# A transformer block in fp32 on one core: the chunk order of a softmax batch, the turn of one output tile, and the queue that issues half of the block swaps

## The chip, the cores and the metric

The kernel runs on one core of a Trainium2 chip. Time is device time in microseconds for one launch, smaller is better; the figure compared is the median of several runs.

## What is computed

An adaptive-layernorm block on x of 2048 rows and 512 columns, all in float32. A vector c gives six modulation rows (shift, scale and gate for each half). The first half is causal attention with 16 heads of 128; the second is a shared gated MLP plus a mixture of 64 experts, of which each row takes 4 (at most 128 rows per expert).

```python
mod = (silu(c) @ wmod).reshape(1, 6, 1, -1)
sa, ca, ga, sb, cb, gb = ...            # ga, gb kept at least 0.25 away from 0
h = layernorm(x) * (1 + ca) + sa
q, k, v = h @ Q_w + Q_b, h @ K_w + K_b, h @ V_w + V_b      # per head
x = x + ga * (softmax(causal(q @ k.T / sqrt(128))) @ v @ O_w + O_b)
h = layernorm(x) * (1 + cb) + sb
x = x + gb * (experts(h, top 4 of softmax(h @ Wr + router_bias)) + shared_mlp(h))
```

## The kernel before

The attention stage fills the span from about 54 us to 1658 us. The 2048 query rows are 16 tiles of 128 rows; two neighbours form a pair, 0 to 7. Pair pr needs 2*pr+1 and 2*pr+2 key blocks of 128. The pairs of a head are worked in five batches, `BATCHES = ((7,), (6,), (5, 0), (4, 1), (3, 2))`, so there are 16 x 5 = 80 steps, written (head, batch) below.

A batch passes through four phases, which are spread over three steps:

- Softmax (`softmax_tile`). A tile's row of logits is cut into chunks of at most 1024 columns. A chunk (pair, tile, number) is multiplied on TensorE (L572) into a PSUM tile `ps`, of which there are two in a ring (tag "sc"). VectorE adds the causal mask to the last 128 columns (L584) and takes the negative maximum (L585; L589 joins that of a tile's first chunk). ScalarE writes the exponential into `p` (L591). When a tile is complete, `normalise` makes its factor (L547 to L554); the scaling itself is done on VectorE (L559, only in batches 0 and 1 for the pair's first tile) or ScalarE (L795). `CHUNKS` lists the order of a batch's chunks.
- Swap (`swap_blocks`, L616). The 32-row groups of `p` are moved to other partitions, as 16 DMAs from SBUF to SBUF of 104 to 124 KB, into a tile `pt`. Part a of `pt`, a = 0 to 3, is written by four of the DMAs; those of parts 0 and 1 are issued first (`half` 0), then those of parts 2 and 3 (`half` 2). `p` and `pt` have two buffers each.
- Turn (`turn_blocks`, L626). VectorE transposes the 32 x 32 blocks of part a in place. There are four turns per batch.
- Weighted values (`weighted_values`, L644). TensorE multiplies the values with `pt` into `po`; ScalarE adds the bias into `at` (L653, one buffer), and GpSimd's queue (POOL) stores it to DRAM as `atd` (L658).

In step n TensorE works on the weighted values of batch n, on the softmax of batch n+2 and on fill work: the q and k products of the next head (`project`, L222) and the value products of the next group (`values`, L447). `merge` writes these streams out as one order by hand: it always takes the next item of the stream whose done share is smallest, and at given shares of the whole it inserts marks. The turns of batch n+1 are the marks 0.58, 0.66, 0.8 and 0.88. The swap of batch n+2 is issued when the step's streams are at their end:

```python
for a, at in enumerate((0.58, 0.66, 0.8, 0.88)):
    marks.append((at, lambda a=a: turn(n + 1, a)))
merge([st for st in streams if st], marks)
if n + 2 < len(steps):
    swap(n + 2)
```

So the softmax of batch 3 (pairs 4 and 1, the first "mixed" row that the change touches) is worked in step (head, 1), and that of batch 2 (pairs 5 and 0) in step (head, 0). Every engine runs its instructions in the order in which they are written. All loads of weights, the swaps and the reloads of `atd` are issued from SP's queue; POOL's queue has the stores of `atd` and of the normed rows, and later the gathers of the expert stage.

The output stage follows (tiles t of 128 rows, 1658 us to about 1830 us). For each tile TensorE adds up 16 products, one per head (L1140); VectorE adds the result to the residual (L1163), and `norm(t)` makes the normed rows h: statistics (L955, L957), square root on ScalarE (L959), then L960 to L966. `turn_h(t)` transposes h on TensorE (L973) and copies it on ScalarE (L974) into `h2T`; `logit(t)` multiplies that with the router's weights (L982); `choose` makes the routing of two tiles. The dictionaries `TURN`, `LOGIT` and so on say after which product (t, hd) of the loop each of these is written. In that loop a `TURN` stands ahead of a `norm` at the same place. `norm(1)`, `norm(2)` and `norm(3)` are written at (4,10), (4,12) and (4,15), `norm(4)` at the end of tile 4, `logit(0)` at (4,14) and `logit(1)` at (5,3).

The expert stage and the shared MLP follow; the change does not touch them.

Of the kernel before, what the change touches and what calls it, by code (L numbers as in the profile page):

```python
# [23 lines left out]
def adaln_block_kernel(  # L24
# [23 lines left out]
    nc = tc.nc  # L48
# [74 lines left out]
    with ExitStack() as att:  # L123
# [386 lines left out]
        def blocks_of(s):  # L510
            return sum(4 * pr + 3 for pr in BATCHES[s])

        def first_block(s, pr):
# [8 lines left out]
            ((7, 1, 0), (7, 1, 1), (7, 0, 0), (7, 0, 1)),  # L522
            ((6, 1, 0), (6, 1, 1), (6, 0, 0), (6, 0, 1)),
            ((5, 0, 0), (0, 0, 0), (5, 0, 1), (5, 1, 0), (0, 1, 0), (5, 1, 1)),
            ((4, 1, 0), (4, 1, 1), (1, 0, 0), (4, 0, 0), (4, 0, 1), (1, 1, 0)),
            ((3, 1, 0), (2, 1, 0), (3, 0, 0), (2, 0, 0)),
        )

# [80 lines left out]
        def swap_blocks(s, pb):  # L609

            w = blocks_of(s) * 32
            pt = ptp.tile([P, PW], F32, name="pt")
            for half, d in [(h, d) for h in (0, 2) for d in range(4)]:
                for a in (half, half + 1):
                    b = (a + d) % 4
                    nc.sync.dma_start(  # L616
                        out=pt[32 * b : 32 * (b + 1), a * w : (a + 1) * w],
                        in_=pb[32 * a : 32 * (a + 1), b * w : (b + 1) * w],
                    )
            return pt  # L620
# [189 lines left out]
        def swap(n):  # L810
            flush()
            flush_shares()
            turned[n] = swap_blocks(steps[n][1], probs.pop(n))
# [156 lines left out]
    def turn_h(t):  # L970
        tp = psO.tile([P, DC, P], F32, name="tp", tag="tr")
        for k in range(DC):
            nc.tensor.transpose(tp[:, k, :], hs_[t][:, k * P : (k + 1) * P], ident)  # L973
        nc.scalar.copy(h2T[:, :, t * P : (t + 1) * P], tp)  # L974
# [122 lines left out]
    table = psO.tile([CAP, 2 * E], F32, name="table", tag="tr")  # L1097
    ALL = ((0, 4), (4, 8), (8, 12), (12, 16))

    TURN = {(4, 10): 0, (5, 0): 1, (5, 4): 2, (5, 9): 3, (6, 1): 4, (6, 8): 5}  # L1100
    LOGIT = {(4, 14): 0, (5, 3): 1, (5, 15): 2, (6, 2): 3, (6, 11): 4, (6, 15): 5}
    POSITION = {(5, 14): 0, (6, 10): 1}
    SEAT = {(6, 5): 0, (7, 0): 1}
    for t in range(7, NT):
        TURN[t, 10] = t - 1
        LOGIT[t, 14] = t - 1
# [4 lines left out]
    with tc.manual_schedule():  # L1111
# [17 lines left out]
        for t in range(NE, NT):  # L1129
# [9 lines left out]
            for hd in range(H):  # L1139
# [7 lines left out]
                if hd == 5:  # L1147
                    nc.vector.tensor_add(acc[:, t, :], acc[:, t, :], ga)
                if (t, hd) in TURN:
                    turn_h(TURN[t, hd])  # L1150
                if (t, hd) in ((4, 10), (4, 12), (4, 15)):
# [419 lines left out]
```

## Time and profile before

| | |
|---|---|
| median of 3 runs | 2384.27 us (2384.24 to 2387.44) |
| the profiled execution | 2396.46 us, span 2394.7 us, granted clock 0.995 |
| TensorE (PE) busy | 2339.7 us, 98% |
| VectorE (DVE) busy | 1548.9 us, 65% |
| ScalarE (ACT) busy | 861.7 us, 36% |
| GpSimd (POOL) busy | 218.9 us, 9% |
| swap DMAs (L616) | 1280, all on SP's queue |
| stores of `atd` (L658) | 128 on POOL's queue |
| DMA queue q1 (SP), q0 (POOL) | 252.74 MB and 54.54 MB |

In the rows of the profile a group is named by line, engine, operation and tiles, output first. A timeline row begins with its start and its duration in us, and in square brackets stand the idle time of its engine before it and what ended that. PEld is TensorE's weight load, SPq and POOLq are the queues' own instructions. The waits list says who waited for whom: total us, times, longest. A share of busy time is a mean over the stages of the span.

### The profile page before, as it was taken

The page shows a single profiled execution, that of the slowest core. Times are in us where ns is not written, and L with a number is a line of the kernel's source. Part 1 is how long each engine was busy: PE and PEld are TensorE (multiplying, and loading weights), DVE is VectorE, ACT ScalarE, POOL GpSimd, SP SyncE. Part 2 cuts the span into 40 slices and gives each one's busy share as a digit, 9 for nine tenths or more (in the row PEclk, how much of TensorE's full clock was granted, in tenths as well). Part 3 has the DMA queues.
Part 4 walks back from the last instruction along what each step waited for, and adds up shares of the span by engine and source line. Part 5 has one row for each costly group of instructions (what it writes and reads, how often), then busy time and mean ns, then how long its engine had stood idle before and what let it go on. Part 6 is the DMA issues. An engine that isn't in the chain of part 4 may idle for free.

```text
span 2394.7 us, 27691 instructions
## 1 busy us (share of the span) xinstructions
PE 2339.7 (98%) x9078; PEld 1504.3 (63%) x9078; DVE 1548.9 (65%) x3100; ACT 861.7 (36%) x1703; POOL 218.9 (9%) x286
## 2 busy tenths in 40 slices
PE   7999999999999999999999999999999999999989
PEld 3666657666576676666766767555444677867734
DVE  5467767677676776776767767764755654634645
ACT  3344444444444444444444444442111222212200
POOL 0000000000000000000000000000000111211163
PEclk9999999999999999999999999999999999999999
DMA  4234544454454454454544445656232578777564
GB/s 141 64 83 117 126 115 115 101 133 112 96 141 104 104 130 97 119 128 99 120 100 116 114 96 147 190 159 195 78 119 84 154 216 245 232 225 239 169 188 135
DMA packets 223835, 325.84 MB, mean 136 GB/s; under 512 B 31894, under 2 KB 138442, under 8 KB 223692
## 3 DMA queue, kind: packets, MB, share of 16 engines
q1 hardware_dynamic: 196812, 252.74, 41.0%
q0 software_dynamic: 17664, 54.54, 7.5%
q10 hardware_dynamic: 9216, 16.78, 1.9%
q8 instruction: 73, 1.20, 0.2%
q14 instruction: 70, 0.57, 0.1%
HBM read 139.39 MB, written 41.95 MB: 76 GB/s over the span
## 4 chain that ended last, share of the span: by engine, by line
PE 86%; DVE 4%; SPq 3%; issue 2%; ACT 1%; DMA 1%; DVEq 0%; ACTq 0%
PE po L644 17%; PE ps L572 17%; PE pqk L222 13%; PE pv L447 7%; PE pso L1140 6%; PE pst L1289 5%; PE pse L1433 5%; PE psd L1351 5%; PE psg L1205 3%; SPq L616 3%; PE psy L1454 2%; PE psb L769 2%; DVE pt L626 1%; PE tpx L1426 1%; PE pv L497 1%
## 5 line engine op out<-in xcount | busy, mean ns | idle before, releaser
L591 ACT ACTIVATE p<-ps,nm 128x1024 f32<-128x1024 f32 (+7 forms) x384 | 331.7, 864 | 854.1 <-DVE nm L589 359.8
L644 PE MATMUL po<-pt,v 128*128 128x256 f32 (+1 forms) x2304 | 564.8, 368 | 3.0 <-DVE pt L626 2.3
L644 PEld LDWEIGHTS po<-pt,v 128*128 128x128 f32 x2304 | 420.9, 191 | 204.6 <-issue 158.0
L572 PE MATMUL ps<-kt,qt 128*128 128x512 f32 (+3 forms) x1280 | 532.2, 530 | 15.2 <-ACT p L591 14.5
L585 DVE TENSOR_REDUCE nm<-ps 128x1 f32<-128x1024 f32 (+7 forms) x384 | 349.9, 911 | 105.5 <-PE ps L572 96.7
L626 DVE STREAM_TRANSPOSE pt<-pt 128x832 f32<-128x832 f32 (+2 forms) x320 | 337.0, 1069 | 21.8 <-DMA pt<-p 16.1
L572 PEld LDWEIGHTS ps<-kt,qt 128*128 128x128 f32 x1280 | 234.9, 190 | 178.4 <-issue 144.0
L795 ACT ACTIVATE p<-p,rs 128x1024 f32<-128x1024 f32 (+3 forms) x320 | 266.0, 860 | 5.3 <-DVE rs L554 5.1
L658 POOL DMA_DIRECT2D atd<-at x128 | 74.3, 584 | 1584.1 <-ACT at L653 1561.2
L1140 PE MATMUL pso<-hT,T 128*128 128x512 f32 x384 | 175.0, 601 | 0.0
L222 PE MATMUL pqk<-T,sw 128*128 128x512 f32 x360 | 169.2, 592 | 0.0
L584 DVE TENSOR_TENSOR ps<-ps,causal 128x128 f32<-128x128 f32 x256 | 72.8, 284 | 111.5 <-PE ps L572 109.7
L1433 PE MATMUL pse<-wgu,xbT 128*128 128x256 f32 x512 | 121.1, 379 | 0.0
L1140 PEld LDWEIGHTS pso<-hT,T 128*128 128x128 f32 x384 | 70.0, 191 | 71.9 <-issue 71.2
L222 PE MATMUL pqk<-hT,wq 128*128 128x512 f32 x240 | 112.8, 592 | 0.0
L1351 PE MATMUL psd<-wsd,hs 128*128 128x512 f32 x256 | 111.5, 592 | 0.0
L222 PEld LDWEIGHTS pqk<-T,sw 128*128 128x128 f32 x360 | 68.4, 190 | 54.1 <-issue 50.2
L1433 PEld LDWEIGHTS pse<-wgu,xbT 128*128 128x128 f32 x512 | 93.8, 190 | 11.7 <-issue 1.0
L1416 POOL DMA_INDIRECT xb<-h2d,tok x64 | 65.0, 1015 | 297.9 <-PE tpx L1426 275.3
L1428 ACT COPY xbT<-tpx 128x512 f32<-128x512 f32 x64 | 37.3, 585 | 145.7 <-DVE y L1456 56.2
L447 PEld LDWEIGHTS pv<-sgb,T 128*128 128x128 f32 x672 | 81.6, 192 | 8.1 <-issue 6.7
L1351 PEld LDWEIGHTS psd<-wsd,hs 128*128 128x128 f32 x256 | 48.6, 190 | 59.0 <-issue 58.6
(423 smaller groups left out, 2648.2 us busy)
## 6 DMA issues: line engine op xcount, KB each, us to landing
pt<-p SPq DMA_DIRECT2D x768, 104.0 KB
pt<-p SPq DMA_DIRECT2D x256, 124.0 KB
pt<-p SPq DMA_DIRECT2D x256, 108.0 KB
atd<-at POOLq DMA_DIRECT2D x128, 128.0 KB
wgu<-in_L_ffn_Wg_dram SPq DMA_DIRECT2D x64, 256.0 KB
wgu<-in_L_ffn_Wu_dram SPq DMA_DIRECT2D x64, 256.0 KB
wd<-in_L_ffn_Wd_dram SPq DMA_DIRECT2D x64, 256.0 KB
ybd<-y ACTq DMA_DIRECT2D x64, 256.0 KB
```

What stands on the lines that cost most here:

```text
L222: nc.tensor.matmul(out=ps, lhsT=l[:, k], rhs=r[:, k], start=(k == 0), stop=(k == 1))
L447: nc.tensor.matmul(out=ps[:, n], lhsT=l[:, k, n * P : (n + 1) * P], rhs=r[:, k], start=(k == 0), stop=(k == 1),)
L572: nc.tensor.matmul(out=ps[:, o : o + wo], lhsT=q, rhs=kts[hd, (c0 + o) // 512][:, :wo], start=True, stop=True,)
L585: nc.vector.tensor_reduce(nm[:, n : n + 1], ps[:, :w], AX.X, ALU.max, negate=True)
L591: nc.scalar.activation(rows[:, r0 + c0 // P : r0 + (c0 + w) // P], ps[:, :w].rearrange("q (r b k) -> q r b k", b=4, k=32), AF.Exp, bias=nm ...
L626: nc.vector.transpose(part, part)
L644: nc.tensor.matmul(out=po if wide else po[:, P:], lhsT=vts[g, kt // 4][:, kt % 4, hh * DH : (hh + 1) * DH], rhs=rows[:, r : r + last + 1 : ...
L795: nc.scalar.activation(part, part, AF.Identity, scale=r)
L1140: nc.tensor.matmul(out=ps, lhsT=abs_[pr][:, hd, i * P : (i + 1) * P], rhs=wos[hd // 4][:, hd % 4, :], start=(hd == 0), stop=(hd == H - 1),)
L1289: nc.tensor.matmul(out=ps[:, h], lhsT=w[:, k, :], rhs=x_[:, k, :], start=k == 0, stop=k == 1,)
L1351: nc.tensor.matmul(out=ps, lhsT=hsh[b, f][:, i * P : (i + 1) * P], rhs=wsd[:, f, :], start=(f == 0), stop=(f == NHC - 1),)
L1433: nc.tensor.matmul(out=ps, lhsT=xts[e][:, k, :], rhs=weights[e][:, k].rearrange("p i h -> p (i h)"), start=(k == 0), stop=(k == DC - 1),)
```

## The change

Three edits.

- In `CHUNKS` the chunks of pair 4 in the batch (4, 1) begin with the pair's first tile instead of its second. The widths of the row, in order, are 1024, 256, 384, 1024, 128, 512 before and 1024, 128, 384, 1024, 256, 512 after; the latter are those of the batch (5, 0).
- In `swap_blocks` the eight DMAs that write parts 2 and 3 are issued from GpSimd's queue, the other eight from SP's as before.
- In `TURN` tile 1 is transposed at (4, 15), after the last product of tile 4, instead of at (5, 0), after the first product of tile 5.

```diff
-            ((4, 1, 0), (4, 1, 1), (1, 0, 0), (4, 0, 0), (4, 0, 1), (1, 1, 0)),
+            ((4, 0, 0), (4, 0, 1), (1, 0, 0), (4, 1, 0), (4, 1, 1), (1, 1, 0)),
...
             for half, d in [(h, d) for h in (0, 2) for d in range(4)]:
+                queue = nc.sync if half == 0 else nc.gpsimd
                 for a in (half, half + 1):
                     b = (a + d) % 4
-                    nc.sync.dma_start(
+                    queue.dma_start(
                         out=pt[32 * b : 32 * (b + 1), a * w : (a + 1) * w],
                         in_=pb[32 * a : 32 * (a + 1), b * w : (b + 1) * w],
                     )
...
-    TURN = {(4, 10): 0, (5, 0): 1, (5, 4): 2, (5, 9): 3, (6, 1): 4, (6, 8): 5}
+    TURN = {(4, 10): 0, (4, 15): 1, (5, 4): 2, (5, 9): 3, (6, 1): 4, (6, 8): 5}
```

## The prediction

> **What bounds the kernel now.** I read the page first, then TensorE's waits, then the timeline around the longest of them. In the page:
>
> ```profile
> PE 2339.7 (98%) x9078; PEld 1504.3 (63%) x9078; DVE 1548.9 (65%) x3100; ACT 861.7 (36%) x1703; POOL 218.9 (9%) x286
> ...
> PE 86%; DVE 4%; SPq 3%; issue 2%; ACT 1%; DMA 1%; DVEq 0%; ACTq 0%
> ```
>
> TensorE is busy 98% and carries 86% of the chain, so an edit can only win time in which TensorE stands still. Its own waits (engine, line, releaser: total us, times, longest):
>
> ```profile
> PE ps L572 <- ACT p L591: 14.5, 16, 1.5
> ...
> PE pl L982 <- ACT h2T L974: 3.4, 2, 3.2
> ```
>
> The first comes once per head (0.8 in most windows of 100 us), the second once in the output stage. The others that the change can reach are "po L644 <- DVE pt L626" (2.3, once) and "po L644 <- issue" (0.7, once). Together 20.9 us: that is the ceiling, unless a slower step hides more. A cross-check from the chain: per head 14 L222 products at 1.72, 7 L447 products at 1.78, 17408 softmax columns at 1.72 per 1024 and L644 at 0.43 per wide and 0.22 per narrow entry (64 and 8) make 95.0 us; heads repeat every 96.28 (POOL's L658 issue at 970.74 and 1067.02). So 1.3 us per head is idle, of which 0.83 is this wait.
>
> The wait in step (4,1) (head 4, batch 1; its softmax stream works for batch 3 of the same head), from the timeline:
>
> ```profile
> 536.35 0.39 PE L572 MATMUL ps<-kt,qt 128*128 128x128 f32 x2
> ...
> 537.22 1.03 DVE L626 STREAM_TRANSPOSE pt<-pt 128x832 f32<-128x832 f32 x1
> ...
> 538.18 0.27 DVE L584 TENSOR_TENSOR ps<-ps,causal 128x128 f32<-128x128 f32 x1
> ...
> 539.00 0.37 ACT L591 ACTIVATE p<-ps,nm 128x128 f32<-128x128 f32 x1 [4.64 <-DVE nm L589]
> ...
> 539.51 1.99 PE L572 MATMUL ps<-kt,qt 128*128 128x512 f32 x4 [0.83 <-ACT p L591]
> ```
>
> The 128-wide chunk (4,0,1) is multiplied at 536.35, but its mask waits on VectorE behind the third product's add (L240) and the fourth transpose (537.22). Its ps buffer, one of two, is free only after the exponential, and the next step's first chunk stands 0.83 us at 539.51.
>
> **Part A, the order of widths.** No instruction is added or removed; six chunks change places. `merge` takes the stream with the smallest done share. The chunks are 1024, 256, 384, 1024, 128, 512 before; the fifth comes due at 2688/3328 = 0.808 of its stream, after the fifth product (0.8) and after all four turns (marks 0.58 to 0.88). After, 1024, 128, 384, 1024, 256, 512 put it at 2560/3328 = 0.769: ahead of the fifth product, the third and the fourth turn. The sixth stays at 0.846.
>
> Rebuilt from the durations above: TensorE starts the 256-wide chunk (4,1,1) at 534.63 - 0.22 = 534.41 and has it at 535.0. VectorE has done two turns and L236 by 535.0, then mask 0.27, maximum 0.42, minimum 0.16: 535.9. ScalarE's exponential and sum, 0.47 + 0.19, free the buffer at 536.6. TensorE comes to the next step after 0.43 + 1.72 + 0.43 + 0.86 + 0.65: 538.5. So 1.9 us of slack stand where 0.83 was short. Step (4,0) already runs these widths: its 256-wide chunk is at 513.98, its exponential at 516.42, the next step's chunk at 518.51 with no wait. The other buffers of the ring have over 1 us. The last scaling before the block swap is 128 columns wider, about 0.1 us of ScalarE, which is 36% busy. Typical waits alone give 16 x 0.83 = 13.3, the row 14.5. I take 14.0.
>
> **Part B, the queues.** Sixteen block transfers per step stay, in the same sizes. SP issues 16 in 10.0 to 10.8 us (0.63 each); now it issues 8 in 5.1, and POOL the 8 that fill parts 2 and 3. POOL's are queued behind the step's atd issue (L658), which waits for the same weighted sums; the next atd issue, 17 to 20 us later, stands behind them and nothing else does until then. SP's later items (weights, wmod, atd reloads) start some 5 us sooner. Step (4,4):
>
> ```profile
> 581.90 1.35 DVE L559 TENSOR_SCALAR p<-p,rs 128x1024 f32<-128x1024 f32 x2
> 582.09 1.28 POOL L658 DMA_DIRECT2D atd<-at  x2 [16.11 <-ACT at L653]
> ...
> 583.39 10.03 SPq L616 DMA_DIRECT2D pt<-p  x16
> ```
>
> POOL is free at 583.37 when SP starts at 583.39; elsewhere it is at most 0.6 us behind (atd until 565.98, SP from 565.36). POOL's price for a swap is not in the trace. Nearest row: a direct copy on POOL takes 539 ns, two in a row 1.07 us. Other end: an indirect gather comes every 1.25 us (0.95 + 0.30 between). I take the direct copy's, 0.54 to 0.6, since a swap is direct; 1.25 stays as the far end. Landing: a pair of atd issues on POOL ended at 1653.73 and SP, which waited for the second, went on at 1655.40, 1.7 later; SP's own swaps land 1.6 to 2.3 after issue. With 2 for both, parts 2 and 3 land about 0.6 + 4.8 + 2 = 7.4 us after the swap's start; before it was 10.1 + 2 = 12.1.
>
> Who uses that? VectorE waits for "DMA pt<-p" 16.1 us in all, 3.4 of it between 130 and 1500, and TensorE almost never. At 1546 to 1548.5 (2.3) the fourth turn is late behind a chunk's maximum rather than the transfer; only about 0.4 goes. At 1651 (0.7) turns 2 and 3 wait for the transfer itself: 0.7 goes. Gain 1.0 (0 to 3.0).
>
> One rule speaks against this part. The row first: beside L559's two scalings the two POOL issues took 1.28 instead of 1.07, and the longest of 128 single ones 764 ns instead of 539. The Trainium skill's "SBUF — State Buffer", section "SBUF: two separate sides", says that a GpSimd-issued DMA cannot write its descriptors while VectorE holds the shared port pair in a two-port mode; its next section gives 620 ns alone and 3100 beside such a copy. By that figure 8 issues could take 25 us, longer than a step of 19; by the trace at worst 6.1. The trace decides, and the swap waits for L559 to end anyway.
>
> **Part C, the second output tile.** Four transposes and one copy move from after tile 5's first product pair to the end of tile 4.
>
> ```profile
> 1679.05 2.74 PE L1140 MATMUL pso<-hT,T 128*128 128x512 f32 x6
> ...
> 1684.36 0.57 ACT L974 COPY h2T<-tp 128x512 f32<-128x512 f32 x1
> ...
> 1684.98 1.10 PE L982 MATMUL pl<-wr,h2T 128*128 128x64 f32 x8 [3.19 <-ACT h2T L974]
> ```
>
> The copy is queued on ScalarE behind the square roots (L959) of tiles 3 and 4, the last of which waits for VectorE until 1684.16. Moved ahead of tile 3's, it finds its input (h of tile 1, done 1675.8) ready; transposes at 1677.7, copy at 1678.4 to 1679.0, before tile 3's square root is due at 1680.06, so nothing behind it waits. The router product at 1681.8 then has its operand. Late next: VectorE's own chain (norm of tile 4, then the routing from 1686.6) doesn't move, so tile 2's copy comes at about 1688.5 and tile 3's transposes wait some 0.2 for its buffer; VectorE's 5.9 us of idle before L1048 takes up the rest. Gain 3.0 (0 to 3.2).
>
> **Sum.** 14.0 + 1.0 + 3.0 = 18.0 us less than this execution's 2396.46 (span 2394.7 and 1.8 around it): 2378.5. That execution lies 12.2 above the median; taken off the median, 2384.3 - 18.0 = 2366.3.
>
> **Rivals.**
> 1. The stall moves along the ring: another chunk meets late VectorE work and half of A's gain stays away, 2366 + 7 = 2373. For: VectorE runs the same 65%, in order. Against: step (4,0) runs the same widths without a wait.
> 2. Bunching. A step's 1.66 MB at q1's rate (252.74 MB in 41.0% of the span, 257 GB/s) needs 6.5 us of the 16 engines, which issue of 10 us spread out. Issued in 5, the first half is slowed by the second. Tightest is step (4,4): 1.98 MB, 7.7 us plus landing 2 = 9.7, and the first turn is due 7.6 after the swap's start. Late by 2.1; about 1 us of cover remains before its ps buffer is asked for (597.35), so I cost it nothing. Without the cover 0.5 to 1 us per head: 2374 to 2382.
> 3. Slower: POOL's issue. Swap, turns, last chunk and next swap form a loop: 0.6 + 8x + 2 + one turn 1.0 + last chunk and its scaling 3.5 (from the fourth turn's end at 538.25 to about 542, less what runs beside) = 7.1 + 8x against a mean step of 19.26. From x = 1.52 us per issue the swaps set the step; from 1.55 the gains of A and C are eaten (17/80 = 0.21 per step). At x = 1.7, 80 x 1.44 - 17 = 98 slower: 2482. Against: 0.54 in the row, and 1.25 even for a gather. For: eight in a row of this shape occur nowhere here.
> 4. The queue change does nothing and A and C hold: 2367, inside the forecast.
>
> **How the numbers follow.** Forecast (with 4) 0.68, rival 1 0.10, rival 2 0.10, rival 3 0.12. About 0.2%, 4.8 us, is what a measurement of this kernel can tell from no change, so faster means under 2379.5 and slower over 2389. Forecast, rival 1 and part of 2 lie below: 0.81. Rival 2's upper end: 0.06. Rival 3, with a worse rival 2: 0.13. The range runs from A, B and C at their upper ends (14.5 + 3.0 + 3.2 = 20.7, with some TensorE idle beyond the row: 2361) to rival 2 without cover (2380); rival 3 stays outside.
>
> **What would show it.** A: "ps L572 <- ACT p L591" gone from TensorE's waits, steps (head,1) 0.8 us shorter; wrong if another wait of L572 comes 16 times. B: L616 as POOL instructions, 640 of about 0.55 us, SP's 8 in about 5; wrong if one takes over 1.5 or VectorE's wait for "DMA pt<-p" grows past 16.1. C: no wait of L982 at tile 5. The whole is wrong if TensorE's busy time falls below 98% of the span.

## The result and the profile after

| | before | after |
|---|---|---|
| median of 4 runs | 2384.26 us (2383.73 to 2387.44) | 2410.12 us (2408.25 to 2412.53) |
| ratio to before, 95% interval | | 1.0106 [1.0089, 1.0124] |
| profiled execution, span | 2396.46, 2394.7 us | 2410.47, 2408.7 us |

The changed kernel is 1.06% slower, some 26 us, where 18 us less was forecast. The queue edit adds a line, so L616 of before is L617 here, L626 is L627, L644 is L645 and L658 is L659.

The page of the changed kernel (engine busy times, the chain's shares, one group of POOL, and the group of turns with its idle time and what ended that):

```profile
PE 2343.6 (97%) x9078; PEld 1503.6 (62%) x9078; DVE 1544.3 (64%) x3100; ACT 860.7 (36%) x1703; POOL 534.1 (22%) x926
...
PE 59%; DVE 15%; DMA 8%; SPq 7%; issue 5%; ACT 3%; POOL 1%; ACTq 0%; DVEq 0%
...
L627 DVE STREAM_TRANSPOSE pt<-pt 128x832 f32<-128x832 f32 (+2 forms) x320 | 337.1, 1069 | 103.8 <-DMA pt<-p 90.7
...
L617 POOL DMA_DIRECT2D pt<-p x640 | 314.7, 499 | 164.4 <-DVE p L559 79.9
```

and the group of turns before:

```profile
L626 DVE STREAM_TRANSPOSE pt<-pt 128x832 f32<-128x832 f32 (+2 forms) x320 | 337.0, 1069 | 21.8 <-DMA pt<-p 16.1
```

TensorE's instructions are the same in number and its busy time grows by only 4 us, yet its share of the chain falls from 86% to 59%: VectorE, the DMAs and SP's queue take 30% of it instead of 8%. The 640 issues on POOL take 499 ns each, so POOL's issuing is not the brake. The line that changed most is that of the turns: VectorE now stands 90.7 us for the swap's data, against 16.1 before.

TensorE's waits after (engine, line, releaser: total us, times, longest):

```profile
PE ps L572 <- ACT p L591: 36.2, 24, 3.3
...
PE po L645 <- DVE pt L627: 3.5, 5, 1.8
...
PE pl L983 <- ACT h2T L975: 0.2, 1, 0.2
```

The wait that part A was to remove is not gone but 2.5 times as long (14.5 before). The one that part C was to remove is down from 3.4 to 0.2. In the stretch from 54 to 1500 us TensorE stands idle 37.6 us instead of 15.3 (1446.0 less a busy time of 1408.37 and 1430.67). Over the whole attention stage, from the first write of `at` to the last, the traces have 1527.2 us before and 1557.2 after.

Where the time goes is seen in the length of the steps, from one batch's write of `at` to the next one's, as a mean over heads 1 to 13, in us. Rows for three of the experiments below are put beside them:

| step | (head,0) | (head,1) | (head,2) | (head,3) | (head,4) | sum |
|---|---|---|---|---|---|---|
| before | 20.43 | 20.71 | 19.67 | 17.06 | 19.36 | 97.23 |
| after | 20.37 | 20.54 | 19.15 | 17.36 | 21.90 | 99.32 |
| A and C, all swaps on SP (e4) | 20.40 | 20.41 | 18.80 | 17.20 | 19.38 | 96.19 |
| queue edit alone (e2) | 20.43 | 20.49 | 19.71 | 17.50 | 21.80 | 99.93 |
| A, C, queue edit in batch 0 only (e10) | 20.25 | 20.43 | 18.84 | 17.04 | 21.78 | 98.34 |

By these marks the order of widths takes 1.04 us from a head, in steps (head,1) and (head,2); the queue edit puts 2.5 us into step (head,4) and some 0.6 elsewhere: 99.32 - 96.19 = 3.13 per head, and 16 heads make 50 us. In the traces the attention stage of after is 45.8 us longer than that of e4 (1557.2 against 1511.4), 36 us of it as idle time of TensorE (40.5 against 4.6).

The marks are writes of ScalarE, and these can come late themselves. TensorE's own idle time between them, as a mean over the same heads, is 0.91 us in (head,1) before and at most 0.05 in any other step. After, (head,1) has none; 0.75 stand in (head,4), 0.27 in (head,3) and 1.60 in (head,0). So TensorE pays for most of what comes late in (head,4) one step later.

Step (4,4) from the timeline of after, with the start of the next step. The swap of batch 0 is issued on both queues, and the first turn of that batch is seen waiting for it:

```profile
591.26 7.58 SPq L617 DMA_DIRECT2D pt<-p  x8
591.70 3.93 POOL L617 DMA_DIRECT2D pt<-p  x8 [0.45 <-issue]
...
601.31 1.21 DVE L627 STREAM_TRANSPOSE pt<-pt 128x992 f32<-128x992 f32 x1 [2.94 <-DMA pt<-p]
602.45 1.19 DVE L585 TENSOR_REDUCE nm<-ps 128x1 f32<-128x1024 f32 x1
603.67 1.11 ACT L591 ACTIVATE p<-ps,nm 128x1024 f32<-128x1024 f32 x1 [5.42 <-DVE nm L585]
...
614.89 0.91 PE L572 MATMUL ps<-kt,qt 128*128 128x384 f32 x2 [1.73 <-ACT p L591]
```

and the same place in before, where the swap had started at 583.39:

```profile
590.97 1.20 DVE L626 STREAM_TRANSPOSE pt<-pt 128x992 f32<-128x992 f32 x1
592.09 1.21 DVE L585 TENSOR_REDUCE nm<-ps 128x1 f32<-128x1024 f32 x1
```

Before, the first turn starts 7.6 us after the swap, with no wait. After, it starts 10.05 us after it. VectorE works in order, so the maximum of the 1024-wide chunk of the next batch stands behind the turn. ScalarE stands 5.42 us for it, and the exponential starts 12.4 us after the swap instead of 9.95 (593.34 in before). The lateness stays on the two engines until a `ps` buffer is asked for that isn't free: TensorE stands 1.73 us at 614.89. In head 5 the turn waits 3.85 (699.77), and TensorE 1.00 at once (703.38) and 1.7 later.

The windows view (us, busy time and instructions of PE, PEld, DVE, ACT, POOL, TensorE's clock, DMA share, GB/s) says why. First before, from the swap's start to the first turn, and on to where the turns have gone on:

```profile
583.40:591.00 7.60, 7.60 (x48) 6.38 (x47) 6.26 (x13) 2.90 (x6) 0.00 (x0) 1.00 0.85 201
591.00:594.60 3.60, 3.60 (x22) 2.94 (x21) 3.51 (x7) 1.26 (x3) 0.00 (x0) 1.00 0.92 206
```

and after, from the swap's start to just before the first turn:

```profile
591.30:600.80 9.50, 9.50 (x56) 7.68 (x56) 6.20 (x12) 2.90 (x6) 3.93 (x8) 1.00 0.83 238
```

With one queue the sixteen DMA engines were already 85 to 92% busy, at 201 to 206 GB/s. With two, 238 GB/s pass in the first 9.5 us. But by the packets of each queue in the traces the swap as a whole gains little: its last packet ends 11.4 us after its start before, and 11.0 after. What changes is which half comes first. Before, SP's first eight DMAs, which bring parts 0 and 1, are through at 6.4 us. After, POOL's eight, parts 2 and 3, are through at 8.7 us, and SP's eight only at 11.0 (over heads 1 to 14 SP's first eight end at 6.4 to 7.7 us before, at 9.7 to 11.0 after). The half that is needed first used to be served first and is now served last. Nobody had waited for the second half.

### The profile page after: what moved, and what is told of

Read it like the earlier page. It is cut to its first block, busy times and chain, and to the rows that moved or that the text cites. A ratio compares the mean times of both kernels' runs of the same rounds, so it can differ in the third digit from the quotient of the medians.

```text
span 2408.7 us, 29006 instructions
## 1 busy us (share of the span) xinstructions
PE 2343.6 (97%) x9078; PEld 1503.6 (62%) x9078; DVE 1544.3 (64%) x3100; ACT 860.7 (36%) x1703; POOL 534.1 (22%) x926
## 4 chain that ended last, share of the span: by engine, by line
PE 59%; DVE 15%; DMA 8%; SPq 7%; issue 5%; ACT 3%; POOL 1%; ACTq 0%; DVEq 0%
PE pqk L222 9%; PE ps L572 9%; PE po L645 8%; DMA pt<-p 8%; PE pso L1141 6%; SPq L617 6%; DVE pt L627 5%; PE pst L1290 5%; PE pse L1434 5%; PE psd L1352 5%; DVE nm L585 4%; PE psg L1206 3%; PE psy L1455 2%; PE psb L770 2%; ACT p L591 2%
## 5 line engine op out<-in xcount | busy, mean ns | idle before, releaser
L591 ACT ACTIVATE p<-ps,nm 128x1024 f32<-128x1024 f32 (+7 forms) x384 | 331.8, 864 | 885.9 <-DVE nm L585 393.9
L572 PE MATMUL ps<-kt,qt 128*128 128x512 f32 (+3 forms) x1280 | 533.5, 533 | 37.2 <-ACT p L591 36.2
L645 PE MATMUL po<-pt,v 128*128 128x256 f32 (+1 forms) x2304 | 564.8, 368 | 4.0 <-DVE pt L627 3.5
L645 PEld LDWEIGHTS po<-pt,v 128*128 128x128 f32 x2304 | 421.9, 190 | 217.4 <-issue 158.5
L627 DVE STREAM_TRANSPOSE pt<-pt 128x832 f32<-128x832 f32 (+2 forms) x320 | 337.1, 1069 | 103.8 <-DMA pt<-p 90.7
L572 PEld LDWEIGHTS ps<-kt,qt 128*128 128x128 f32 x1280 | 232.0, 191 | 197.1 <-issue 136.9
L617 POOL DMA_DIRECT2D pt<-p x640 | 314.7, 499 | 164.4 <-DVE p L559 79.9
L659 POOL DMA_DIRECT2D atd<-at x128 | 75.4, 592 | 1135.2 <-ACT at L654 1117.5
L796 ACT ACTIVATE p<-p,rs 128x1024 f32<-128x1024 f32 (+4 forms) x320 | 266.0, 860 | 5.1 <-DVE rs L554 5.1
```

The costliest lines, as they stand in the source:

```text
L572: nc.tensor.matmul(out=ps[:, o : o + wo], lhsT=q, rhs=kts[hd, (c0 + o) // 512][:, :wo], start=True, stop=True,)
L591: nc.scalar.activation(rows[:, r0 + c0 // P : r0 + (c0 + w) // P], ps[:, :w].rearrange("q (r b k) -> q r b k", b=4, k=32), AF.Exp, bias=nm ...
L617: queue.dma_start(out=pt[32 * b : 32 * (b + 1), a * w : (a + 1) * w], in_=pb[32 * a : 32 * (a + 1), b * w : (b + 1) * w],)
L627: nc.vector.transpose(part, part)
L645: nc.tensor.matmul(out=po if wide else po[:, P:], lhsT=vts[g, kt // 4][:, kt % 4, hh * DH : (hh + 1) * DH], rhs=rows[:, r : r + last + 1 : ...
L796: nc.scalar.activation(part, part, AF.Identity, scale=r)
```

## The experiments

The experiments ran on three chips, and the kernel before was timed beside each group: its median was 2397.87 us beside e1 to e4, 2396.41 beside e5 to e8, 2383.69 beside e9 to e12 and 2398.82 beside e13. So only ratios to the before of the same group are compared. All edits are given relative to before; "A and C" stands for the order of widths and the `TURN` edit together. Theory 1 is throughout that the first half of batch 0's swap lands late and holds VectorE's queue. Its rival, theory 2, is in e1 to e4 that the order of widths only moves the stall, and after them that it is the POOL queue itself that costs.

**Each edit by itself (e1 to e4).**

```diff
e1:  the row of CHUNKS for batch (4, 1), as in the change
e2:  + queue = nc.sync if half == 0 else nc.gpsimd   (and queue.dma_start)
e3:  (5, 0): 1 -> (4, 15): 1 in TURN
e4:  e1 and e3, all swaps on nc.sync
```

> The new order of widths alone; queues and turn as before. Theory 1 (the loss lies in the queues: both halves of a swap share the 16 DMA engines, so the first half lands later): this edit keeps its forecast gain, the wait of L572 on the exponential (14.5 us, 16 times) is gone, 2370 to 2373 us. Theory 2 (the order of widths only moves the stall to another chunk, and the queues are innocent): no gain or a loss, 2384 to 2410, with L572 waiting at another place 16 times.

> The queues alone; order and turn as before. Theory 1: all of the loss and more, since the two gains are missing: the steps (head, 4) 2 to 3 us longer each, 2384 + 16 x 2.5 = 2424 us (2415 to 2432). Theory 2: within 5 us of the kernel before.

> The earlier turn of tile 1 alone. Both theories: the router product's wait of 3.2 us is gone, 2381 us (2380 to 2384.5). If the turn only moves a wait, no change.

> Order of widths and turn, all swaps on SP. Theory 1: 2384 - 14 - 3 = 2367 us (2365 to 2371). Theory 2: 2381 or slower.

Measured: e1 2381.92, 0.9932 [0.9917, 0.9947]. e2 2441.2, 1.0175 [1.0156, 1.0194]. e3 2391.89, 0.9972 [0.9962, 0.9981]. e4 2373.92, 0.9897 [0.9880, 0.9914]. The wait of L572 for "p L591" is down to 1.0 us in e1 and stands at 44.6 us, 38 times, in e2. So the whole loss is the queue edit's; A and C both gain, somewhat more than was expected, and their product, 0.9904, is what e4 shows. Against e4 the full change is 1.0106 / 0.9897 = 1.021 (about 0.0025 either way, if the two intervals are independent): the queue edit costs some 50 us.

**Where the queue edit costs (e5, e10).** On top of A and C, the edit is kept from batch 0, and then made in batch 0 alone.

```diff
e5:  + queue = nc.gpsimd if half == 2 and s > 0 else nc.sync
e10: + queue = nc.gpsimd if half == 2 and s == 0 else nc.sync
```

> New order and turn; the second halves go to POOL only in batches 1 to 4, the widest swap (batch 0, 124 KB per transfer) stays on SP. Theory 1 (the halves share the 16 DMA engines; only the tightest first turn, that of batch 0 in step (head, 4), has no cover): nearly all of the loss is gone, ratio to the kernel before 0.990 to 0.996 where order and turn alone gave 0.990. Theory 2 (the POOL queue costs in every step): four fifths of the loss stay, 1.005 to 1.008.

> New order and turn; only the swap of batch 0 is split over SP and POOL, the other four are on SP. Theory 1: the loss of the changed kernel less what the four other swaps cost (0.993 against 0.990 when they alone were split), so 1.005 to 1.009. If the loss needs all swaps to be split: below 1.0.

Measured: e5 2380.73, 0.9933 [0.9917, 0.9950], as theory 1 had it; e10 2391.48, 1.0037 [1.0022, 1.0051], a little under what was expected. Against e4 that is 0.4% for four batches and 1.4% for one, of 2.1% for all five: batch 0 carries most of it. In e10 step (head,4) has its 21.78 us and the others their length without the edit (the table above). In e5 the traces show no loss in the attention stage: 1511.8 us against 1511.4 of e4, and 96.13 per head against 96.19. So the two parts don't add up: per head e10 loses 2.15 us, e5 nothing and both together 3.13. Where the rest comes from when all five are split, and the 0.4% of e5, stay open. The DMA issues of e10 show the two kinds of swap in one kernel (KB each, median us from issue to landing), and those of after the split swaps of 104 KB:

```profile
pt<-p SPq DMA_DIRECT2D x768, 104.0 KB, 2.2
...
pt<-p SPq DMA_DIRECT2D x128, 124.0 KB, 5.1
pt<-p POOLq DMA_DIRECT2D x128, 124.0 KB, 4.9
```

```profile
pt<-p SPq DMA_DIRECT2D x384, 104.0 KB, 4.0
pt<-p POOLq DMA_DIRECT2D x384, 104.0 KB, 3.8
```

A DMA of 104 KB lands 2.2 us after its issue when its swap is on one queue and some 4 us after it when the swap is split; one of 124 KB in a split swap takes 5 us, whichever queue it came from. Issued sooner, it is in flight for longer instead.

**Which half, and which queue (e6, e7, e8).** On top of A and C: the halves exchange their queues; all on POOL; the second half on ScalarE's queue.

```diff
e6: + queue = nc.gpsimd if half == 0 else nc.sync
e7: + queue = nc.gpsimd
e8: + queue = nc.sync if half == 0 else nc.scalar
```

> New order and turn; the queues exchanged: POOL issues the halves that fill parts 0 and 1, SP those of parts 2 and 3. Theory 1 (equal sharing): the first parts land as late as before the exchange, 1.005 to 1.016. Theory 3 (POOL's packets get ahead and SP's wait for them): the first parts now come early, 0.990 to 0.997.

> New order and turn; all 16 transfers of a swap are issued from POOL, in the old order, at 0.5 us each. Theory 1: what hurts is that both halves are in flight together; in one queue the first half goes first again, 0.987 to 0.996, perhaps below order and turn alone since POOL issues faster than SP. Theory 2 (the POOL queue is slow by itself): worse than with half of them, 1.02 or more.

> New order and turn; the second halves are issued from ScalarE's queue instead of POOL's. Theory 1: the same bunching from another queue, 1.005 to 1.016, and up to 80 x 8 x 0.6 = 384 us of ScalarE's time on top, some of which may show. Theory 2: no bunching without POOL; only ScalarE's issues cost, 0.990 to 1.002.

e7: 2386.24, 0.9963 [0.9949, 0.9977]. All 1280 swap DMAs come from POOL's queue, twice as many as in the change, and the kernel is faster than before: the POOL queue as such is not the cause. The first turn of the same batch 0 (577.10 to 584.31 us) comes 7.2 us after the swap's start with no wait. It is still 0.7% slower than all on SP, but not in every head: heads 1 to 13 take 96.26 us each, against 96.19 in e4, and head 14 takes 104.6 instead of 95.5. There SP reloads `atd` beside POOL's swap, at a DMA share of 0.84 and then 1.02 (0.67 and 0.52 in e4), and TensorE waits for late turns twice, 8.1 us in all.

e6: 2395.85, 0.9999 [0.9990, 1.0008], half of the loss gone, between what the theories said. POOL issues its eight in 3.95 us while SP takes 6.81, and POOL's half is again through first: its last packet ends at 8.5 us, SP's at 9.6. As POOL's is now the first half, the first turn comes 8.7 us after the start and waits 1.61:

```profile
582.23 6.81 SPq L617 DMA_DIRECT2D pt<-p  x8
582.66 3.95 POOL L617 DMA_DIRECT2D pt<-p  x8 [0.45 <-issue]
590.94 1.21 DVE L627 STREAM_TRANSPOSE pt<-pt 128x992 f32<-128x992 f32 x1 [1.61 <-DMA pt<-p]
```

e8: 2692.59, 1.1245 [1.1224, 1.1265]. Neither theory had this, and the run tells nothing between them: ScalarE issues eight DMAs among its exponentials, and these stand behind them: at 583.67 us the eight take 5.66 us, and the next exponential starts at 589.53, after 7.25 us of idle time. ScalarE's waits in e8:

```profile
ACT p L591 <- DMA pt<-p: 554.1, 79, 9.7
```

**What the late turn holds up (e9).** All three edits of the change stand, and the turns are moved to later marks in the steps of batch 4, where batch 0 is turned. The chunk's maximum then stands ahead of the first turn.

```diff
-                    for a, at in enumerate((0.58, 0.66, 0.8, 0.88)):
+                    for a, at in enumerate((0.72, 0.78, 0.86, 0.88) if s == 4 else (0.58, 0.66, 0.8, 0.88)):
```

> The changed kernel (all three edits), and in the steps of batch 4 the first two turns are written later, at 0.72 and 0.78 of the step instead of 0.58 and 0.66, so that the maximum of chunk (6,0,0) stands ahead of the first turn on VectorE. Theory 1a (the late first half costs because that maximum is queued behind the waiting turn, and with it the ps buffer): most of the loss is gone, ratio to the kernel before 0.992 to 0.999 where the changed kernel had 1.011. Theory 1b (the late half costs by itself, through the turns and the weighted values of the next step): 1.008 to 1.015.

Measured 2384.53, 1.0004 [0.9995, 1.0013], between the two expectations; step (head,4) is 20.12 us. About half of the loss is back. The maximum behind the turn is a part of the cost; what the later turns themselves delay, or what the swap's traffic does beside it, is the rest, and this run doesn't part them.

**The same lateness without POOL (e11).** On top of A and C, all on SP, the 16 DMAs are issued in an order that mixes the halves, so that part 0 is complete only with the 13th.

```diff
-            for half, d in [(h, d) for h in (0, 2) for d in range(4)]:
-                for a in (half, half + 1):
+            for d in range(4):
+                for a in range(4):
```

> New order and turn; all 16 transfers on SP, but in the order part 0, 1, 2, 3, part 0, 1, ... instead of first parts 0 and 1, then 2 and 3; no POOL queue. Part 0 is complete after the 13th issue instead of the 7th, 3.8 us later. Theory 1 (what counts is when part 0 has landed, whichever queue brings it): a loss like that of the second queue, 1.003 to 1.015. Theory 2 (POOL's descriptors or its queue slow the engines): as order and turn alone, 0.988 to 0.992.

Measured 2457.57, 1.0309 [1.0292, 1.0327], a larger loss than was expected. No second queue, no POOL, and step (head,4) has 21.74 us, as after. From its timeline:

```profile
601.44 10.03 SPq L616 DMA_DIRECT2D pt<-p  x16
...
611.35 1.21 DVE L626 STREAM_TRANSPOSE pt<-pt 128x992 f32<-128x992 f32 x1 [3.56 <-DMA pt<-p]
```

The first turn comes 9.9 us after the start, like the 10.05 of the change, and costs batch 0 the same. The other batches lose here too (steps (head,0) and (head,1) are 21.15 and 21.58 long); part 0 is issued late in each of them, and VectorE waits 206.0 us for the swaps.

**The second half held back (e12, e13).** On top of A and C, POOL's half stays on POOL but is issued later: a copy of a chunk's maximum on GpSimd stands ahead of it, so that it can't start before that is computed. e12 holds all batches; e13 splits and holds batch 0 alone, until the maximum of chunk (6,1,1).

```diff
+            nc.gpsimd.tensor_copy(held, latest[0])   # the newest maximum
+            swap_blocks(steps[n][1], probs.pop(n), (2,), turned[n])
...
e12: + marks.append((0.35, lambda: late_half(n + 1)))
e13: + if s == 4 and n + 1 < len(steps):
     +     marks.append((0.5, lambda: late_half(n + 1)))
```

> New order and turn, second halves on POOL, but held: POOL first copies one column of the maximum of a chunk at 0.35 of the next step, so its eight issues start some 5 to 7 us after SP's. Theory 1: the first half has the 16 engines for itself again, 0.989 to 0.998, a little lost where parts 2 and 3 now come late. Theory 2: no better than the changed kernel, 1.008 to 1.015.

> New order and turn; only the swap of batch 0 is split, and POOL's half is held until the maximum of chunk (6,1,1) in step (head, 4) is there, some 6 us after SP's start. Against the split of batch 0 without a hold (1.0037). Theory 1 (both halves in flight at once make the first late): the first turn's wait is gone, step (head, 4) back to about 19.5 us, ratio 0.988 to 0.996. Theory 2 (POOL's queue costs by itself): 1.000 to 1.006.

e12 measured 2438.85, 1.0236 [1.0216, 1.0257], outside both expectations and slower than the change itself. It is a poor test: in the steps that matter the hold missed. In step (head,4) the maximum it waits for was early, POOL started at 598.97, only 2.0 us after SP, and the turn waited 3.04 us as in the change; in other batches POOL started up to 9.5 us after SP, which made the last turns late, for which TensorE waited ("po L647 <- DVE pt L629", 24.3 us). e13 puts the hold where it was meant:

```profile
580.43 4.95 SPq L618 DMA_DIRECT2D pt<-p  x8
586.44 0.18 POOL L823 COPY held<-nm 128x1 f32<-128x1 f32 x1 [6.38 <-DVE nm L589]
587.34 3.93 POOL L618 DMA_DIRECT2D pt<-p  x8 [0.72 <-DMA pt<-p]
587.66 1.20 DVE L628 STREAM_TRANSPOSE pt<-pt 128x992 f32<-128x992 f32 x1
590.54 1.21 DVE L628 STREAM_TRANSPOSE pt<-pt 128x992 f32<-128x992 f32 x1
593.80 2.30 DVE L628 STREAM_TRANSPOSE pt<-pt 128x992 f32<-128x992 f32 x2 [1.03 <-DMA pt<-p]
```

It measured 2393.75, 0.9971 [0.9958, 0.9984], against 1.0037 of e10, which differs from it only in the hold. Same queues and same bytes, the second half starts 6.9 us after the first: SP's eight issues take 4.95 us again and are through at 6.35 us, the first turn is at 7.2 us with no wait, and step (head,4) falls from 21.78 to 20.20. It is just above theory 1's numbers and below theory 2's. In heads 1 to 13 that is 1.55 of the 2.15 us that e10 loses per head against e4; in the whole kernel only about half of the loss is back. The rest of the way to e4 is at least in part the hold's own: the third turn waits 1.03 us above, and in head 14 TensorE stands 5.5 us for a turn that the hold made late.

The best version is e4, the change without its queue edit: 0.9897 [0.9880, 0.9914], faster than both kernels.

## Why the prediction was wrong

**Part A was right.** 14.0 us were forecast (a ratio of 0.994); e1 measured 0.9932, some 16 us, and the wait of L572 fell from 14.5 to 1.0. TensorE's idle time in step (head,1) went from 0.91 us to none, where 0.8 was forecast; the marks of the table show most of it one step later. Rival 1 didn't come.

**Part C was right in its mechanism and too small.** The wait of L982 falls from 3.4 to 0.2, as forecast with 3.0. The ratio of e3 is worth 6.7 us [4.6, 9.1] of 2398. The traces show where the excess is. From the last write of `at` to the first product of the experts (L1433) it is 239.2 us in before and e2 and 240.9 in e1, the three kernels without this edit, and 234.8 in e3, 234.7 in after and 234.1 in e4: 4.4 to 6.8 us less. In before the granted clock is halved for 3.4 us right behind the wait, from 1686.2 us on (it is 0.72 as a mean from 1684 to 1690), and products of 592 ns take 1061 there. That is another 1.7 us. Behind the same wait e2 has 3.4 us of halved clock and e1 6.8; none of the twelve traces with the edit has any in this stage. The forecast priced the wait and put the slower clock behind it at nothing.

**Part B failed.** Its price for POOL was near: 0.54 to 0.6 forecast, 0.499 measured, eight in 3.93 us, and the longest of the 640 took 0.711, nothing like the 3.1 that was weighed against this part; so rival 3 is out. The first step that failed is "With 2 for both, parts 2 and 3 land about 0.6 + 4.8 + 2 = 7.4 us after the swap's start". It carried the landing time of an unhurried DMA, 2 us, over to DMAs issued twice as fast, as if the swap were bound by its issue. The DMAs of the split swap land 5 us after their issue (e10). The engines were already 85 to 92% busy in this stretch of the trace of before, a number that the prediction doesn't use. Parts 2 and 3 were through 2.7 us sooner, at 8.7 instead of 11.4 us, and parts 0 and 1, which VectorE was waiting for, 4.6 us later. The prediction's own sign of being wrong came: VectorE's wait for the swaps grew from 16.1 to 90.7.

**Rival 2 named the mechanism and the place, and its price was mis-sized.** It said step (4,4) and a first turn late by 2.1 us. Measured are 2.5 us there (10.05 against 7.6, with a wait of 2.94 on VectorE), and a wait of 3.85 in the next head. The span-mean rate of 257 GB/s was too fast for the swap, whose bytes passed at 207 over its whole length; and it let the two halves share evenly, where POOL's half was through first. The step that decided the result is "about 1 us of cover remains before its ps buffer is asked for (597.35), so I cost it nothing". A lateness of 2.1 exceeds a cover of 1.0 in the prediction's own figures. And the cover of one buffer isn't the measure: VectorE's queue runs in order, and of the 3 us that it loses at 601.31 TensorE still pays 1.73 at 614.89, in the next step. The cost was put at 0.5 to 1 us per head without cover; it is 3.1 per head for the whole edit, and 2.15 when batch 0 alone is split (e10).

**Summed up:** by the ratios -16 (A), -7 (C) and +50 (B) make some 27, and in the traces -15.8 and +45.8 in the attention stage and -4.5 behind it make 25.5. Measured were 26; forecast were -14, -3 and -1.

Shown by runs: that the loss is the queue edit's (e2, e4), mostly batch 0's (e5, e10), that a POOL queue alone doesn't cause it and that a first part issued late on SP alone costs batch 0 the same (e7, e11), and that more than two thirds of batch 0's loss per head leaves when the second half is held back (e13). Open: what the split of the other four batches adds to that of batch 0; e9's other half; and some 10 us by which TensorE's busy time in the attention stage is longer in after than in e4 for the same 6037 instructions, of which longer stretches of halved clock (10.2 us against 3.4) explain about 3.4. Why POOL's half gets through first was not tested beyond e6.

## What to carry to other kernels

Before a transfer is split over two queues, read the DMA share of that stage, not of the span: here, at 0.85 to 0.92, a second queue brought the whole only 0.4 us of 11.4 sooner and changed who came first. Where one half is needed first, the order of issue on a single queue protected it. And a late operand on an engine that works in order is priced by what is queued behind it, over the next steps too, not by the slack of the one buffer beside it.

## What was not expected of the hardware

- An issue of these DMAs is quicker on POOL (eight in 3.93 us) than on SP (eight in 4.95 in e13, where they run alone). Beside POOL's issues SP's eight take 7.58 us in step (4,4), and a single one took 1.70.
- With equal bytes, and issued 0.4 us later, POOL's half of a split swap is through before SP's: at 8.7 against 11.0 us in after, and at 8.5 against 9.6 in e6, where the halves are exchanged. Two queues move 238 GB/s in the first 9.5 us, against 201 to 206 from one; over the whole swap it is 207 against 198.
- DMAs on ScalarE's queue hold up its arithmetic, 554.1 us in e8: some 7 us at each of 79 swaps, of which the issuing takes 5.7 in the one shown.
- A wait at L1205 in the last stage goes with the chip and not with the kernel. It is 1.0 to 3.1 us in the four traces of e9 to e12, taken where before runs in 2383.69 us, and 9.2 to 15.7 in those of e1 to e8 and e13, where before runs in 2396 to 2399. The trace of before has 12.1 and that of after 1.7, so these two are not alike here: from the first product of the experts to the end it is 496.8 and 484.1 us. That is why the two profiled spans differ by 14.0 us and the medians by 26. The cause of the wait is open.
